# Convolution weights brought in unexpanded on 32 partitions and spread by ScalarE, in a group-norm and convolution kernel

## The chip, the cores and the metric

The kernel runs on one core of one Trainium2 chip. The metric is the device time of one execution in microseconds (us). The kernel before took 87.22 us, the median of three runs (86.58, 87.22 and 87.36). The profile shown below was taken from one more execution, which took 86.55 us; from its first to its last instruction it spans 84.8 us. TensorE, VectorE, ScalarE, GpSimd and SyncE are called PE, DVE, ACT, POOL and SP in the profile. A DMA is issued by an engine's queue (here SP's) and then moves data on the core's 16 DMA engines.

## The reference

The input `x` is 8 images of 32 channels and 128 x 128 pixels, float32. Each image is group-normalised (16 groups of two channels), convolved with a 3 x 3 weight of 32 x 32 channels, given a bias, and added to `x`. The convolution goes through a 256-point FFT, and its output window starts at offset 64:

```python
def _L0_conv_ref(x, weight, bias, stride, padding):
    # ... zero-pad x and weight to 256 x 256, multiply their FFTs, transform back to sp ...
    sh = (fft_H - out_h) // 2            # 64
    sw = (fft_W - out_w) // 2            # 64
    out = sp[:, :, sh:sh + out_h, sw:sw + out_w]
    return out + bias[None, :, None, None]

def _gn(v, G=16, eps=1e-5):              # mean and variance over two channels and all pixels
    # ...
    return ((g - m) / jnp.sqrt(s + eps)).reshape(v.shape)

x = x + _L0_conv_ref(_gn(x), L0_conv_weight, L0_conv_bias, 1, 1)
```

Output pixel (i, j) is therefore the full convolution at (i + 64, j + 64). It is different from the bias alone only for i and j up to 65, and it needs only the lower right corner of the image.

## The kernel before

The host splits every image by the parity of row and column: partition `q*32 + c`, with q = 2 x (row parity) + (column parity), holds channel c, as 64 x 64 values. So an image is a tile of 128 x 4096 floats, 2 MB. Eight such tiles stand in SBUF at once; every image has its own, is changed in place, and is stored from it. All loads and all stores are issued by SP, on one queue.

```python
    xts = [xpool.tile([P, H, W], F32, name=f"x{img}") for img in range(B)]
    wb_sb = cpool.tile([P, 4 * P + 1 + NSIGN], F32, name="wb_sb")   # 128 x 521 floats
    bias_sb = wb_sb[:, 4 * P : 4 * P + 1]
    signs = wb_sb[:, 4 * P + 1 :]
    for img in range(B):
        pieces = (4, 4) if img < 2 else (8,)       # images 0 and 1 in two halves
        # ...
            nc.sync.dma_start(xts[img][:, rows, :], x[img, :, rows, :])
        # ...
        if img == 0:
            nc.sync.dma_start(wb_sb, wb)
```

The 3 x 3 convolution of the parity-split image is four matmuls with 128 x 128 weight blocks, accumulated in PSUM, one for each pair (dr, dc) of shifts by 0 or 1. The blocks are built on the host: each tap of the 32 x 32 x 3 x 3 weight stands in several 32 x 32 squares of them, and the other squares are zero.

While data arrives, POOL makes a pattern and DVE makes from it the matrix `avg`, which averages over a group. PE runs matmuls into a spare bank before there is anything real to do (`keep_warm`). ACT loads its table with one early `Sqrt`. Then every image goes through these steps:

```python
    def take_stats(img, first, last):     # DVE, eight pieces of an image
        # ...
            nc.vector.bn_stats(stats[img][:, s, :], ...)

    def aggregate(img):                   # DVE, then two small ACT instructions
        nc.vector.bn_aggr(mv, stats[img].rearrange("p n s -> p (n s)"))
        nc.scalar.activation(terms[:, 0:NSIGN], signs, AF.Identity, scale=mv[:, 0:1])
        nc.scalar.activation(terms[:, NSIGN:], mv[:, 1:2], AF.Identity, bias=eps, scale=float(FFT * FFT))

    def group(img):                       # PE: averages over the group
        nc.tensor.matmul(ps_ms[img], avg, mvs[img], start=True, stop=True)

    def normalize(img):                   # small ACT and DVE steps, then g on ACT
        # ... square, var, std, rstd ...
            nc.scalar.activation(g[:, rows, :], xt[...], AF.Identity,
                                 bias=rstd[:, 1:2], scale=rstd[:, 0:1])

    def add_bias(img):                    # ACT: where the convolution is zero
        nc.scalar.activation(low, low, AF.Identity, bias=bias_sb)
        nc.scalar.activation(right, right, AF.Identity, bias=bias_sb)

    def multiply(img, n):                 # PE: four matmuls for a chunk of 11 rows
        # ...
            nc.tensor.matmul(ps[...], wb_sb[:, k * P : (k + 1) * P], g[...],
                             start=(k == 0), stop=(k == 3))

    def add(img, first, last):            # DVE: x + convolution + bias, in place
        nc.vector.scalar_tensor_tensor(..., scalar=bias_sb, ...)

    def store(img, first, last):
        nc.sync.dma_start(out[img, :, first:last, :], xts[img][:, first:last, :])

    keep_warm(0, 3)
    take_stats(0, 0, NSTAT)
    aggregate(0); group(0); keep_warm(0, 2); normalize(0); add_bias(0)
    take_stats(1, 0, NSTAT)
    for img in range(B):
        # ... multiply(img), aggregate/group/normalize/add_bias of img + 1,
        #     add and store of img - 1, statistics of img + 2 ...
    store(B - 1, N, H)
    add(B - 1, 0, 2)
    store(B - 1, 0, 2 * ROWS)
    add(B - 1, 2, NCHUNK)
    store(B - 1, 2 * ROWS, N)
```

The order of instructions on every engine is the order of the program. A DMA issue waits for the DMA eight issues earlier, whose completion counter it uses again.

Of the kernel before, what the change touches and what calls it, by code (L numbers as in the profile page):

```python
# [24 lines left out]
F32 = mybir.dt.float32  # L25
AF = mybir.ActivationFunctionType
ALU = mybir.AluOpType

P = 128
# [4 lines left out]
NSIGN = 8  # L34
# [3 lines left out]
def conv_preact_kernel(  # L38
# [6 lines left out]
    nc = tc.nc  # L45

    B, _, H, W = x.shape
    C = P // 4
    LO = (FFT - 2 * H) // 4 - 1
    N = H - LO  # L50
# [4 lines left out]
    cpool = ctx.enter_context(tc.tile_pool(name="const", bufs=1))  # L55
# [4 lines left out]


    xts = [xpool.tile([P, H, W], F32, name=f"x{img}") for img in range(B)]
    wb_sb = cpool.tile([P, 4 * P + 1 + NSIGN], F32, name="wb_sb")
    bias_sb = wb_sb[:, 4 * P : 4 * P + 1]
    signs = wb_sb[:, 4 * P + 1 :]
    for img in range(B):
        pieces = (4, 4) if img < 2 else (8,)
        first = 0
        for piece in pieces:
            rows = slice(first, first + piece * STATS)  # L70
            nc.sync.dma_start(xts[img][:, rows, :], x[img, :, rows, :])
            first += piece * STATS
        if img == 0:
            nc.sync.dma_start(wb_sb, wb)


    pair = cpool.tile([P, P // 2, 2], F32, name="pair")
# [6 lines left out]
        out=pair, in_=pair, pattern=[[2, P // 2], [0, 2]], base=1,  # L84
        channel_multiplier=-1, compare_op=ALU.is_ge, fill=0.0,
    )
    eps = cpool.tile([P, 1], F32, name="eps")
    nc.vector.memset(eps, EPS * FFT * FFT)
    pair2 = pair.rearrange("p a b -> p (a b)")
# [5 lines left out]

    warm = cpool.tile([P, 1], F32, name="warm")
    nc.scalar.activation(warm, eps, AF.Sqrt)  # L97

    gs = [cpool.tile([P, N, N], F32, name=f"g{k}") for k in range(2)]
    stats = [cpool.tile([P, NSTAT, 6], F32, name=f"stats{img}") for img in range(B)]  # L100
# [53 lines left out]
    def multiply(img, n):  # L154
        g = gs[img % 2]
        if n == 0:

            pss[img] = ps_conv.tile([P, NCHUNK, BANK], F32, tag="ps", name=f"ps{img}")
        ps = pss[img][:, n, 0 : ROWS * N].rearrange("p (r w) -> p r w", w=N)
        for k in range(4):  # L160
            dr, dc = k // 2, k % 2

            rows = min(ROWS, N - dr - n * ROWS)
            top = n * ROWS + dr
            nc.tensor.matmul(  # L165
                ps[:, 0:rows, 0 : N - dc], wb_sb[:, k * P : (k + 1) * P],
                g[:, top : top + rows, dc:N],
                start=(k == 0), stop=(k == 3),
            )
# [30 lines left out]
    for img in range(B):  # L200
        more = img + 1 < B
        multiply(img, 0)
        multiply(img, 1)
        if more:
            aggregate(img + 1)
        if img:
            add(img - 1, 0, NCHUNK)
            if img == 1:
                store(0, N, H)
                store(0, 0, N)  # L210
            else:
                store(img - 1, 0, H)
        if more:
            group(img + 1)
            normalize(img + 1)
            add_bias(img + 1)
        multiply(img, 2)
        if img + 2 < B:
            take_stats(img + 2, 0, NSTAT)
# [55 lines left out]
```

## Time and profile before

| What | Value |
|---|---|
| time, median of three | 87.22 us (86.58 to 87.36) |
| span of the profile | 84.8 us |
| PE busy | 66.1 us (78%), 218 instructions |
| DVE busy | 54.6 us (64%) |
| ACT busy | 48.5 us (57%), 82 instructions |
| POOL busy | 1.8 us (2%) |
| moved by DMA | 33.87 MB in 3172 packets, mean 399 GB/s |
| of it `wb_sb` | 260.5 KB, one DMA |

Shares of busy time are averages over the whole span. The profile also cuts the span into slices, and gives for each the busy share of every engine and of the DMA engines; it follows the chain of work that ended last back from the last instruction; and it lists how long each DMA took from its issue to its landing. A DMA's landing time holds its waiting in the queue too, behind what was issued earlier.

### The profile page before, as it was taken

How to read it: one execution, taken by the hardware profiler on the slowest of the kernel's cores; microseconds unless marked ns; L12 is line 12 of the kernel's file. 1: busy time of each engine (PE TensorE's matmuls, PEld its weight loads, DVE VectorE, ACT ScalarE, POOL GpSimd, SP SyncE). 2: the span in 40 equal slices, each digit the busy share in tenths (PEclk: the TensorE clock that was granted, in tenths of full speed). 3: DMA queues.
4: the chain of work that ended last, by engine and by line, in shares of the span. 5: the costliest groups of instructions: out<-in, count | busy, mean ns of one | idle time of the engine just before them, and what ended most of it. 6: DMA issues, size and time to landing. Idle time of an engine off the chain costs nothing.

```text
span 84.8 us, 732 instructions
## 1 busy us (share of the span) xinstructions
PE 66.1 (78%) x218; PEld 40.1 (47%) x218; DVE 54.6 (64%) x103; ACT 48.5 (57%) x82; POOL 1.8 (2%) x7
## 2 busy tenths in 40 slices
PE   0009968999999999999999999999999999500000
PEld 0014323666666666666666676666666666100000
DVE  0319938973998899699799969969992600420000
ACT  6000037984994897599489769948967980000000
POOL 6200000000000000000000000000000000000000
PEclk9999999999999999999999999999999999985555
DMA  2899999999999999999999999999999999999970
GB/s 39 294 425 413 435 429 471 417 448 409 448 394 456 409 433 421 440 409 433 317 404 426 472 417 448 409 456 402 456 409 448 417 448 417 433 417 402 414 318 17
DMA packets 3172, 33.87 MB, mean 399 GB/s; under 512 B 352, under 2 KB 352, under 8 KB 992
## 3 DMA queue, kind: packets, MB, share of 16 engines
q1 hardware_dynamic: 3168, 33.82, 95.1%
q8 instruction: 2, 0.03, 0.1%
q14 instruction: 2, 0.02, 0.0%
HBM read 17.04 MB, written 16.78 MB: 399 GB/s over the span
## 4 chain that ended last, share of the span: by engine, by line
PE 70%; DVE 8%; DMA 6%; ACT 2%; DVEq 1%; issue 0%
PE ps L165 68%; DMA x<-x_dram 6%; DVE stats L105 6%; PE ps_m L124 1%; DVE x L174 1%; ACT g L141 1%; DVEq L270 1%; DVE mv L113 0%; ACT std L136 0%; ACT terms L115 0%; ACT square L132 0%; ACT rstd L139 0%; ACT terms L116 0%; DVE rstd L138 0%; DVE var L133 0%
## 5 line engine op out<-in xcount | busy, mean ns | idle before, releaser
L165 PE MATMUL ps<-g,wb_sb 128*128 128x363 f32 (+1 forms) x192 | 58.7, 462 | 0.3 <-ACT g L141 0.3
L165 PEld LDWEIGHTS ps<-g,wb_sb 128*128 128x128 f32 x192 | 35.3, 189 | 20.5 <-ACT g L141 2.7
L105 DVE BATCH_NORM_STATS2 stats<-x 128x6 f32<-128x512 f32 x64 | 38.7, 677 | 2.7 <-DMA x<-x_dram 2.6
L150 ACT ACTIVATE x<-x,wb_sb 128x1984 f32<-128x1984 f32 x8 | 15.6, 1949 | 0.3
L174 DVE SCALAR_TENSOR_TENSOR x<-ps,wb_sb,x 128x1089 f32<-128x1089 f32 (+2 forms) x9 | 10.5, 1180 | 7.2 <-PE ps L165 7.2
L141 ACT ACTIVATE g<-x,rstd 128x396 f32<-128x396 f32 (+1 forms) x16 | 12.7, 838 | 0.3
L190 PE MATMUL ps_w<-x,avg 128*128 128x512 f32 x10 | 7.1, 864 | 6.2 <-DMA x<-x_dram 6.2
L152 ACT ACTIVATE x<-x,wb_sb 128x1023 f32<-128x1023 f32 x8 | 9.1, 1132 | 0.0
L115 ACT ACTIVATE terms<-wb_sb,mv 128x8 f32<-128x8 f32 x8 | 2.4, 301 | 10.9 <-DVE mv L113 10.9
L190 PEld LDWEIGHTS ps_w<-x,avg 128*128 128x128 f32 x10 | 2.5, 273 | 8.7 <-issue 8.7
L124 PEld LDWEIGHTS ps_m<-terms,avg 128*128 128x128 f32 x16 | 3.0, 190 | 3.4 <-ACT terms L116 1.9
L132 ACT ACTIVATE square<-ps_m 128x7 f32<-128x7 f32 x8 | 1.4, 177 | 5.2 <-PE ps_m L124 5.2
L133 DVE COPY var<-ps_m 128x1 f32<-128x1 f32 x8 | 1.3, 158 | 4.6 <-ACT square L132 4.6
L136 ACT ACTIVATE std<-var 128x1 f32<-128x1 f32 x8 | 2.4, 295 | 1.8 <-DVE var L133 1.8
L138 DVE RECIPROCAL rstd<-std 128x1 f32<-128x1 f32 x8 | 1.3, 164 | 2.9 <-ACT std L136 2.9
L113 DVE BATCH_NORM_AGGREGATE mv<-stats 128x2 f32<-128x48 f32 x8 | 3.0, 372 | 0.3
L139 ACT ACTIVATE rstd<-ps_m,rstd 128x1 f32<-128x1 f32 x8 | 2.1, 261 | 1.8 <-DVE rstd L138 1.8
L124 PE MATMUL ps_m<-terms,avg 128*128 128x9 f32 x16 | 2.4, 222 | 0.7 <-ACT terms L116 0.7
L116 ACT ACTIVATE terms<-mv,eps 128x1 f32<-128x1 f32 x8 | 2.2, 279 | 0.0
L97 ACT ACT_TABLE_LOAD x1 | 1.3, 1283 | 0.8 <-PEq L263 0.8
L132 ACT ACTIVATION_READ_ACCUMULATOR square<-ps_m 128x1 f32 x8 | 1.6, 194 | 0.0
L91 DVE TENSOR_TENSOR avg<-pair 128x64 f32<-128x64 f32 x1 | 0.2, 226 | 1.7 <-POOL pair L83 1.7
(11 smaller groups left out, 2.8 us busy)
## 6 DMA issues: line engine op xcount, KB each, us to landing
x<-x_dram SPq DMA_DIRECT2D x6, 2048.0 KB, 26.1
out_dram<-x SPq DMA_DIRECT2D x6, 2048.0 KB, 13.7
x<-x_dram SPq DMA_DIRECT2D x4, 1024.0 KB, 8.4
out_dram<-x SPq DMA_DIRECT2D x2, 992.0 KB, 21.2
out_dram<-x SPq DMA_DIRECT2D x1, 1056.0 KB, 22.4
out_dram<-x SPq DMA_DIRECT2D x1, 704.0 KB, 8.7
out_dram<-x SPq DMA_DIRECT2D x1, 352.0 KB, 9.1
wb_sb<-wb_dram SPq DMA_DIRECT2D x1, 260.5 KB, 7.5
```

The lines of the kernel that those rows point to most:

```text
L105: nc.vector.bn_stats(stats[img][:, s, :], xts[img][:, STATS * s : STATS * (s + 1), :].rearrange("p h w -> p (h w)"),)
L113: nc.vector.bn_aggr(mv, stats[img].rearrange("p n s -> p (n s)"))
L115: nc.scalar.activation(terms[:, 0:NSIGN], signs, AF.Identity, scale=mv[:, 0:1])
L124: nc.tensor.matmul(ps_ms[img], avg, mvs[img], start=True, stop=True)
L132: nc.scalar.activation(square, contrasts, AF.Square, accum_out=var[:, 0:1])
L136: nc.scalar.activation(std, var[:, 0:1], AF.Sqrt, bias=var[:, 1:2])
L141: nc.scalar.activation(g[:, rows, :], xt[:, LO + rows.start : LO + rows.stop, LO:W], AF.Identity, bias=rstd[:, 1:2], scale=rstd[:, 0:1],)
L150: nc.scalar.activation(low, low, AF.Identity, bias=bias_sb)
L152: nc.scalar.activation(right, right, AF.Identity, bias=bias_sb)
L165: nc.tensor.matmul(ps[:, 0:rows, 0 : N - dc], wb_sb[:, k * P : (k + 1) * P], g[:, top : top + rows, dc:N], start=(k == 0), stop=(k == 3),)
L174: nc.vector.scalar_tensor_tensor(part.rearrange("p (n r) w -> p n r w", r=ROWS), in0=pss[img][:, first:last, 0 : ROWS * N].rearrange("p n ...
L190: nc.tensor.matmul(ps_w, avg, piece, start=True, stop=True)
```

## The change

The weights, the biases and the sign patterns are no longer laid out on the host for 128 partitions. The host sends the weight as it is, input channel first (32 x 288 floats), and beside it for each of the four quarters of the partitions its column of biases and its eight columns of signs (32 x 36 floats): 32 rows of 324 floats, 41 KB in place of 260.5 KB. This is loaded once, on partitions 0 to 31, between the two halves of image 0 (before: after both). On the chip POOL fills a tile `w_sb` of 128 x 512 floats with zero. Then 20 ACT instructions, five for each quarter, copy the bias and sign columns and the taps to the quarter's partitions and to their places in the four blocks. They stand in ACT's order after the early `Sqrt` and ahead of image 0's first real step. The matmuls then read `w_sb`, and the bias and the signs come from the small tile `bs_sb`. The change is for moving fewer bytes.

```diff
-    wb_sb = cpool.tile([P, 4 * P + 1 + NSIGN], F32, name="wb_sb")
-    bias_sb = wb_sb[:, 4 * P : 4 * P + 1]
-    signs = wb_sb[:, 4 * P + 1 :]
+    wb_sb = cpool.tile([C, 9 * C + 4 * (1 + NSIGN)], F32, name="wb_sb")
     ...
             nc.sync.dma_start(xts[img][:, rows, :], x[img, :, rows, :])
+            if img == 0 and first == 0:
+                nc.sync.dma_start(wb_sb, wb)
             first += piece * STATS
-        if img == 0:
-            nc.sync.dma_start(wb_sb, wb)
     ...
+    w_sb = cpool.tile([P, 4 * P], F32, name="w_sb")
+    nc.gpsimd.memset(w_sb, 0.0)
     ...
+    bs_sb = cpool.tile([P, 1 + NSIGN], F32, name="bs_sb")
+    bias_sb, signs = bs_sb[:, 0:1], bs_sb[:, 1:]
+    taps = wb_sb[:, 0 : 9 * C].rearrange("p (a b o) -> p a b o", a=3, b=3)
+    w6 = w_sb.rearrange("p (dr dc r q o) -> p dr dc r q o", dr=2, dc=2, r=2, q=2)
+    places = {
+        0: ((0, slice(0, 1), slice(2, 3)), (1, slice(0, 2), slice(0, 2))),
+        1: ((0, slice(0, 2), slice(1, 3)), (1, slice(1, 2), slice(0, 1))),
+    }
+    for rin in range(2):
+        for cin in range(2):
+            q = 2 * rin + cin
+            to = slice(q * C, (q + 1) * C)
+            of = 9 * C + q * (1 + NSIGN)
+            nc.scalar.activation(bs_sb[to, :], wb_sb[:, of : of + 1 + NSIGN], AF.Identity)
+            for dr, r, a in places[rin]:
+                for dc, c, b in places[cin]:
+                    nc.scalar.activation(w6[to, dr, dc, r, c, :], taps[:, a, b, :], AF.Identity)
     ...
-                ps[:, 0:rows, 0 : N - dc], wb_sb[:, k * P : (k + 1) * P],
+                ps[:, 0:rows, 0 : N - dc], w_sb[:, k * P : (k + 1) * P],
     ...
-    blocks = np.zeros((2, 2, C, 2, 2, 2, 2, C), weight.dtype)
     ... the host's loops that filled the blocks ...
-                blocks.reshape(4 * C, 16 * C),
-                np.tile(np.asarray(L0_conv_bias).reshape(C, 1), (4, 1)),
-                signs,
+                weight.transpose(1, 2, 3, 0).reshape(C, 9 * C),
+                np.concatenate(
+                    [np.broadcast_to(np.asarray(L0_conv_bias).reshape(C, 1), (4, C, 1)),
+                     signs.reshape(4, C, NSIGN)],
+                    axis=2,
+                ).transpose(1, 0, 2).reshape(C, 4 * (1 + NSIGN)),
```

More of the change, by code (lines that the diff above doesn't have):

```diff
@@ L234 @@
     weight = np.asarray(L0_conv_weight)
-    blocks = np.zeros((2, 2, C, 2, 2, 2, 2, C), weight.dtype)
-    for dr, rin, rout in np.ndindex(2, 2, 2):
-        a = rout + 2 - 2 * dr - rin
-        for dc, cin, cout in np.ndindex(2, 2, 2):
-            b = cout + 2 - 2 * dc - cin
-            if 0 <= a <= 2 and 0 <= b <= 2:
-                blocks[rin, cin, :, dr, dc, rout, cout, :] = weight[:, :, a, b].T
     bits = [(-1.0) ** (np.arange(4 * C) // k % 2) for k in (2 * C, C, 1)]
```

## The prediction

> **What bounds the kernel now.** I read the chain of work that ended last first, because it names a bound, and then looked for what it leaves out.
>
> ```profile
> PE 70%; DVE 8%; DMA 6%; ACT 2%; DVEq 1%; issue 0%
> ...
> 63.71 9.53 PE ps L165 x32
> 73.24 0.02 issue
> 73.26 0.97 DVE x L174
> 74.24 0.50 DVEq L270
> ```
>
> The reader is to see that the shares add up to only 87%, and that the chain stops at 74.74 us in a span of 84.8. The last 10 us have no compute instruction in them: they are the last stores. So the next views are the slices and the busy time by stage (columns: stretch and its length; PE, PEld, DVE, ACT and POOL busy; the granted clock; the share of the DMA engines; GB/s).
>
> ```profile
> DMA  2899999999999999999999999999999999999970
> ...
> 4.00:42.00 38.00, 34.83 (x110) 20.44 (x111) 30.66 (x56) 24.25 (x44) 0.00 (x0) 1.00 1.01 425
> 44.00:82.00 38.00, 29.22 (x103) 18.40 (x102) 21.48 (x37) 21.28 (x33) 0.00 (x0) 0.92 1.01 428
> ...
> 78.00:80.00 2.00, 0.00 (x0) 0.00 (x0) 0.00 (x0) 0.00 (x0) 0.00 (x0) 0.50 0.99 418
> 80.00:82.00 2.00, 0.00 (x0) 0.00 (x0) 0.00 (x0) 0.00 (x0) 0.00 (x0) 0.50 1.00 411
> 82.00:84.00 2.00, 0.00 (x0) 0.00 (x0) 0.00 (x0) 0.00 (x0) 0.00 (x0) 0.50 0.18 69
> ```
>
> The DMA engines are full from about 4 us until 82 us, at 425 to 428 GB/s, in the half with the loads as in the half with the stores. PE is nearly as full from 14.5 to 73.2 us, but PE is not what the end waits for. The test is how long each late store stays in the queue:
>
> ```profile
> 63.81 0.33 SPq L182 DMA_DIRECT2D out_dram<-x  x1
> out_dram<-x SPq DMA_DIRECT2D x1, 2048.0 KB, 10.4
> ...
> out_dram<-x SPq DMA_DIRECT2D x1, 704.0 KB, 8.7
> ```
>
> The very first load, with an empty queue before it, took 5.2 us for 1024 KB, of which about 2.45 us is moving at 428 GB/s; some 2.8 us is the way there and back. A 2048 KB store alone would then take 4.9 + 2.8 = 7.7 us, and 704 KB 1.7 + 2.8 = 4.5 us. The real ones took 10.4 and 8.7 us, so they waited 2.7 and 4.2 us behind others. The other whole-image stores took 11.4 us and more. So computing could be up to about 2.7 us later everywhere, and the DMA engines would still never run dry. **The bound is the stream of bytes, 33.87 MB, on the DMA engines**; everything else fits inside it.
>
> **What the Trainium skill says.** Four places bear on this. "DMA: Bandwidth & Descriptors", "Where 436 GB/s comes from", puts the ceiling of the 16 engines at 435 GB/s; the trace's 425 and 428 GB/s are 98% of that, so nothing but fewer bytes shortens the stream. The same page, "Why a DMA increments its semaphore by 16 and not by 1", says that a DMA is divided over the largest number of engines, up to 16, that divides its slowest dimension: 128 rows are then 8 per engine, and 32 rows are 2 per engine. No view here shows the division. Its section "Queues, rings and completion order" says that each engine takes its queue's descriptors in order, so a load put earlier delays all behind it by its own length; the landings of the trace are in the order of issue. "ScalarE: Activation LUTs", "What ACT_TABLE_LOAD costs", gives an activation of N elements per partition as 186 ns + 0.833 ns x N when scale and bias are immediate, 93 ns more for each operand that is a pointer, and 93 ns of overlap back to back. The trace agrees:
>
> ```profile
> L150 ACT ACTIVATE x<-x,wb_sb 128x1984 f32<-128x1984 f32 x8 | 15.6, 1949 | 0.3
> ...
> L132 ACT ACTIVATE square<-ps_m 128x7 f32<-128x7 f32 x8 | 1.4, 177 | 5.2 <-PE ps_m L124 5.2
> ```
>
> The rule gives 279 + 1653 = 1932 ns for the first, with one pointer (measured 1949), and 192 ns for the second, with none (177). In the timeline the two instructions that make `terms` start at 11.47 and 11.68 us while the first is 0.30 us long: they overlap by 0.09 us.
>
> **The change, part by part.**
>
> *Fewer bytes.* The old load is 128 x 521 x 4 = 266,752 bytes, the new one 32 x 324 x 4 = 41,472. What the old one cost the stream is read from SP's issues, because the last three loads wait for the landing of the DMA eight issues earlier:
>
> ```profile
> 6.06 0.33 SPq L71 DMA_DIRECT2D x<-x_dram  x1
> 8.55 0.33 SPq L71 DMA_DIRECT2D x<-x_dram  x1
> 9.20 0.33 SPq L71 DMA_DIRECT2D x<-x_dram  x1
> ```
>
> They were released by the first half of image 0, its second half, and `wb_sb`. The second half took 2.49 us, `wb_sb` 0.65 us. The new load has a quarter of the rows per engine, each 1296/2084 = 0.62 as long: 0.65 x 0.25 x 0.62 = 0.10 us; rows of 1296 bytes are a little dearer per byte, so I take 0.12 us. **Saved on the stream: 0.65 - 0.12 = 0.53 us.** By bytes alone it is 0.225 MB / 428 GB/s = 0.53 us too. This lies on the path that sets the end, and comes back in full.
>
> *The load's new place.* It now goes ahead of image 0's second half, which lands about 0.12 us later, at 8.67 in place of 8.55 us. DVE finishes the first half's statistics at 8.54 us (6.07 + 2.47 in the chain), so all of the front of the computation may start 0.12 us later. The slack of 2.7 us takes that: cost at the end 0.
>
> *The zero fill on POOL.* A fill of 128 x 128 took 0.205 us; four times that is at most 0.8 us, from 2.6 to 3.4 us. ACT needs it only when the weights land. Cost 0.
>
> *Twenty copies on ACT.* A quarter has one copy of 9 elements and four of 32, 64, 64 and 128: 297 elements, 1188 in all. By the rule above a copy takes 93 ns + 0.833 ns x N in a row: 20 x 0.093 + 1188 x 0.000833 = 1.86 + 0.99 = 2.85 us. They begin when the small load lands, at about 6.06 + 0.12 = 6.2 us, and end at 9.1 us. ACT is idle there: its `terms` instruction waits until DVE's aggregate ends at 11.45 us (its longest idle stretch is 9.2 us). **All 2.85 us lie in that gap, with 2.4 us to spare. Cost 0.**
>
> *Sum.* -0.53 us, everything else beside it. 87.22 - 0.53 = 86.69; I say **86.7 us**, 0.6% less.
>
> **The rivals.**
>
> First, *ACT comes too late*. With no overlap and with pointer operands, a copy is 279 ns + 0.833 ns x N: 5.58 + 0.99 = 6.57 us, ending at 12.8 us, 1.3 us after the aggregate. The first matmul would start 1.3 us later, and so would everything on PE. The overlap in the trace speaks against it. Even so the slack is 2.7 us before and about 2.2 us after (the stream being 0.5 us shorter), so the time would still be near 86.7 us. Only if the copies took over 7.4 us would the end move; at 10 us in all, about 89 us.
>
> Second, *PE is the real bound*, as the chain's 70% suggests. Then fewer bytes bring nothing, the front is 0.1 us later, and the time is 87.3 us. Against it stand the 10 us of stores after PE's end, and the 10.4 us that a store waits.
>
> Third, *the saved bytes are filled elsewhere*: there is a dip to about 300 GB/s at 41 to 43 us, where the stream turns from loads to stores, and the DMA engines do not all end together (69 GB/s from 82 to 84 us). If the small load is put on fewer engines, say four rows on each of eight, those eight save 0.65 - 0.24 = 0.41 us only. That makes 86.8 us.
>
> **Range and chances.** The effect is 0.4 to 0.65 us by the steps above. The three runs before differ by 0.78 us among themselves, which is more than the effect, and a median of three can be off by half of that. So 86.1 to 87.3 us should hold it eight times in ten. Faster by 2% would need 1.74 us, three times what the load's whole removal could give: 0.02. Slower by 2% needs the first rival at its worst: 0.03. Within 2%: 0.95.
>
> **What would show each step right or wrong.** In the profile after: 96 packets fewer (3172 to about 3076) and 33.64 MB; SP's load that waits for `wb_sb` issued at about 6.2 us and the one that waits for image 0's second half at 8.67 us; the third landing thus 0.5 us sooner than before; 20 copies on ACT of mean 0.24 us that end by 9.1 us; an idle ACT until DVE's aggregate; PE's first convolution at 14.5 to 14.7 us and its last end at 73.2 to 73.5 us; the late stores' landing times 0.5 to 0.7 us shorter than 8.7 and 10.4; the span at 84.3 us. I am wrong if PE's end moves by over 2 us, if the copies are longer than 0.35 us each, or if the stream's dip at the turn from loads to stores becomes longer.

## The result, and the profile after

The changed kernel takes **85.91 us**, the median of six runs (85.57 to 86.13), against 87.20 us before (86.58 to 87.36). The ratio is 0.9865, with a 95% interval of 0.9824 to 0.9906: 1.3 us less, where 0.53 us was predicted. All ratios below leave out executions over 1.5% above their kernel's fastest; as the kernel before spreads by more than that, its ratios are nearer to 1 than those of the medians, and I give both.

The page of the changed kernel shows the smaller load as expected, and DMA engines that are as full as before:

```profile
span 83.9 us, 752 instructions
...
DMA  2899999999999999999999999999999999999990
...
DMA packets 3075, 33.63 MB, mean 401 GB/s; under 512 B 352, under 2 KB 384, under 8 KB 896
```

The 20 copies, in the groups by form (number, then busy us, mean ns of one, idle before and its releaser):

```profile
L118 ACT ACTIVATE w_sb<-wb_sb 32x64 f32<-32x64 f32 x8 | 1.7, 238 | 0.0
L118 ACT ACTIVATE w_sb<-wb_sb 32x128 f32<-32x128 f32 x4 | 1.2, 292 | 0.0
L118 ACT ACTIVATE w_sb<-wb_sb 32x32 f32<-32x32 f32 x4 | 0.8, 211 | 0.0
L115 ACT ACTIVATE bs_sb<-wb_sb 32x9 f32<-32x9 f32 x4 | 0.8, 210 | 4.2 <-DMA wb_sb<-wb_dram 4.2
```

The last of them and what follows, in ScalarE's timeline:

```profile
9.07 0.70 ACT L118 ACTIVATE w_sb<-wb_sb 32x128 f32<-32x128 f32 x4
11.75 0.30 ACT L136 ACTIVATE terms<-bs_sb,mv 128x8 f32<-128x8 f32 x1 [1.98 <-DVE mv L134]
```

They run from 6.46 to 9.77 us and ScalarE then sits idle for 1.98 us: hidden. The late stores, shown for before at 10.4 and 8.7 us, are the surprise. Their issue in the timeline, and their landing in the table of DMAs:

```profile
64.15 0.33 SPq L203 DMA_DIRECT2D out_dram<-x  x1
```

```profile
out_dram<-x SPq DMA_DIRECT2D x1, 2048.0 KB, 9.0
...
out_dram<-x SPq DMA_DIRECT2D x1, 704.0 KB, 7.4
```

Both are issued 0.34 us later than before (64.15 and 74.64 us) and land 1.1 and 1.0 us earlier. That is more than the stream was shortened by. The end of the span, by stage (the last two numbers are the share of the DMA engines and GB/s; one engine of 16 is 0.06), first before:

```profile
82.00:83.00 1.00, 0.00 (x0) 0.00 (x0) 0.00 (x0) 0.00 (x0) 0.00 (x0) 0.50 0.31 124
83.00:84.00 1.00, 0.00 (x0) 0.00 (x0) 0.00 (x0) 0.00 (x0) 0.00 (x0) 0.50 0.04 14
```

and after:

```profile
81.00:82.00 1.00, 0.00 (x0) 0.00 (x0) 0.00 (x0) 0.00 (x0) 0.00 (x0) 0.50 0.72 287
82.00:83.00 1.00, 0.00 (x0) 0.00 (x0) 0.00 (x0) 0.00 (x0) 0.00 (x0) 0.50 0.07 28
```

The last stretch shown holds about one engine's work after (0.07) and less before (0.04): the end is set by the **last** of 16 engines, not by the stream as a whole. The trace marks the completion of each DMA on each engine, 16 marks a DMA. Below, the mean mark is the mean over the 16 marks of the last store, and the lag is how far the last of them comes after it. The marks of the last store have a mean of 82.75 us before and 82.18 after (0.57 less, the forecast's 0.53), and the last of them comes 1.13 us after that mean before, and 0.72 after. So there are two gains: the bytes, and an end with less lag. The second one is what the experiments are about.

### The profile page after: what moved, and what is told of

The parts are those of the page before. It is cut to its first block, busy times and chain, and to the rows that moved or that the text cites. A ratio compares the mean times of both kernels' runs of the same rounds, so it can differ in the third digit from the quotient of the medians.

```text
span 83.9 us, 752 instructions
## 1 busy us (share of the span) xinstructions
PE 66.3 (79%) x218; PEld 40.1 (48%) x218; DVE 54.5 (65%) x103; ACT 51.8 (62%) x102; POOL 2.3 (3%) x8
## 2 busy tenths in 40 slices
DMA packets 3075, 33.63 MB, mean 401 GB/s; under 512 B 352, under 2 KB 384, under 8 KB 896
## 4 chain that ended last, share of the span: by engine, by line
PE 70%; DVE 8%; DMA 7%; ACT 2%; issue 1%; DVEq 1%; ACTq 0%
PE ps L186 69%; DMA x<-x_dram 7%; DVE stats L126 6%; PE ps_m L145 2%; DVE x L195 1%; ACT g L162 1%; DVEq L287 1%; DVE mv L134 0%; ACT std L157 0%; ACT terms L136 0%; ACT square L153 0%; ACT rstd L160 0%; ACT terms L137 0%; DVE rstd L159 0%; DVE var L154 0%
## 5 line engine op out<-in xcount | busy, mean ns | idle before, releaser
L186 PE MATMUL ps<-g,w_sb 128*128 128x363 f32 (+1 forms) x192 | 58.7, 462 | 0.4 <-ACT g L162 0.4
L186 PEld LDWEIGHTS ps<-g,w_sb 128*128 128x128 f32 x192 | 35.3, 189 | 20.6 <-ACT g L162 1.6
L171 ACT ACTIVATE x<-x,bs_sb 128x1984 f32<-128x1984 f32 x8 | 15.6, 1950 | 0.3
L195 DVE SCALAR_TENSOR_TENSOR x<-ps,bs_sb,x 128x1089 f32<-128x1089 f32 (+2 forms) x9 | 10.5, 1179 | 7.2 <-PE ps L186 7.2
L173 ACT ACTIVATE x<-x,bs_sb 128x1023 f32<-128x1023 f32 x8 | 9.1, 1132 | 0.0
L136 ACT ACTIVATE terms<-bs_sb,mv 128x8 f32<-128x8 f32 x8 | 2.4, 301 | 3.7 <-DVE mv L134 3.7
L115 ACT ACTIVATE bs_sb<-wb_sb 32x9 f32<-32x9 f32 x4 | 0.8, 210 | 4.2 <-DMA wb_sb<-wb_dram 4.2
L118 ACT ACTIVATE w_sb<-wb_sb 32x64 f32<-32x64 f32 (+2 forms) x16 | 2.8, 244 | 0.0
```

Source lines behind the costliest of these rows:

```text
L118: nc.scalar.activation(w6[to, dr, dc, r, c, :], taps[:, a, b, :], AF.Identity)
L186: nc.tensor.matmul(ps[:, 0:rows, 0 : N - dc], w_sb[:, k * P : (k + 1) * P], g[:, top : top + rows, dc:N], start=(k == 0), stop=(k == 3),)
L195: nc.vector.scalar_tensor_tensor(part.rearrange("p (n r) w -> p n r w", r=ROWS), in0=pss[img][:, first:last, 0 : ROWS * N].rearrange("p n ...
```

## The experiments

Bytes, place of the load and ScalarE's longer program change together in this diff. The theories: all of the gain is **bytes**; the rest comes from the load's **place**; the rest comes from the **program**, whose instructions are fetched through the same DMA engines. Medians of the kernel before were 87.03, 87.20, 86.96 and 87.02 us in the four sets of runs.

**Repeats.** Both kernels once more, unchanged.

> The kernel before, run once more as it is, for a second trace of it. Every theory: ratio 1.00, 87.2 us. If the last DMA engine's lag is an accident of one execution, its second trace ends its stores at another time than 83.9 us; if it belongs to the program, the instruction fetch at about 71 us and the end near 83.9 us come again.

> The changed kernel once more as it is. All theories: near 85.9 us, if the first measurement was typical. Its trace shows whether the mean of the 16 engines' last completions (82.18 us in the first trace, 82.75 before) and the lag of the last engine behind that mean (0.72 us, against 1.14 before) come again: the mean should, to 0.1 us; by the theory that the lag is an accident of each execution, the lag should lie elsewhere between 0.7 and 1.7 us.

Before: 87.09 us, ratio 0.9998 (0.9967 to 1.003). Its one trace, of an execution of 87.38 us, has the last mark at 84.50 us and no instruction fetch near 71 us, so neither came again; nothing below is built on so long an execution. After: 85.88 us, ratio 0.9888 (0.9829 to 0.9947). Its mean mark is 82.17 us and its lag 0.78 us. The mean came again to 0.01 us and the lag to 0.06, so in the changed kernel neither is an accident of one execution.

**Old size at the new place, with the copies.**

```diff
-    wb_sb = cpool.tile([C, 9 * C + 4 * (1 + NSIGN)], F32, name="wb_sb")
+    wb_sb = cpool.tile([P, 521], F32, name="wb_sb")     # rows and columns beyond 32 x 324 are unused
     ... the copies read wb_sb[0:C, ...]; the host pads the array with zeros ...
```

> The changed kernel, but its one load has the old size again, 128 rows of 521 floats (only 32 x 324 of them are used), at the new place. Bytes alone (all of the 1.3 us come from the bytes): 87.2 us, the gain is gone. Bytes and program (0.53 us from bytes, the rest from another instruction stream and the lag of the last DMA engine): 86.4 to 86.5 us. Place (the rest comes from the load's new place): 86.4 us too; the run with the load moved alone tells these two apart.

86.49 us, ratio 0.9985 (0.996 to 1.001); mean mark 82.66, lag 0.98 us. Against the changed kernel's 85.9 us the bytes are worth 0.6 us, and by the medians something else is worth the other 0.5. By the ratio alone the bytes would carry all but 0.15%. The mean mark is on the side of before.

**No copies, small load.** All matmuls run, on zero weights; bias and signs are ones.

```diff
-    for rin in range(2): ...          # the 20 copies
+    nc.gpsimd.memset(bs_sb, 1.0)
```

> The changed kernel without the 20 copies: the small load stays, the weights stay zero and the bias and sign columns are filled with one by POOL, so the convolution is left out in value but every matmul runs. ScalarE's program has its old length. Bytes alone or place: 85.9 us as the changed kernel, since the copies are hidden. Bytes and program: 86.6 us, with an instruction fetch late in the trace as in the kernel before.

86.19 us, ratio 0.9922 (0.9888 to 0.9957), mean mark 82.24, lag 1.01 us: between the two expectations. Leaving the copies out gains nothing, as it should if they are hidden, and the mean follows the bytes.

**Program alone.**

```diff
     nc.scalar.activation(warm, eps, AF.Sqrt)
+    spare = cpool.tile([P, C], F32, name="spare")
+    for _ in range(20):
+        nc.scalar.activation(spare, avg[:, 0:C], AF.Identity)
```

> The kernel before with 20 extra ScalarE instructions (128 x 32, into a tile nobody reads) after the early Sqrt, done before image 0's statistics end. Bytes and place are those of before. Bytes alone or place: 87.2 us. Bytes and program: 86.4 to 86.5 us, with no instruction fetch near 71 us and a last DMA engine that lags less (1.2 us in place of 1.65 us from first to last engine).

87.02 us, ratio 1.0013 (0.998 to 1.0046): the length of ScalarE's program by itself does nothing to the time. That theory, in this form, fell.

**Place alone, and size alone.**

```diff
+            if img == 0 and first == 0:
+                nc.sync.dma_start(wb_sb, wb)
             first += piece * STATS
-        if img == 0:
-            nc.sync.dma_start(wb_sb, wb)
```

> The kernel before with its 260.5 KB load issued between the two halves of image 0, nothing else changed. Place theory (the load's place takes some 0.5 us off the last engine's lag, whatever its bytes): 86.5 us, as the changed kernel with the big load had. Program theory (the longer ScalarE program does it, together with the place or by how instruction fetches fall): 87.0 us as before. The mean of the last completions stays at 82.7 us by both.

The same edit the other way round, in the changed kernel:

> The changed kernel with its small load issued after both halves of image 0, where the old load stood. Bytes theory: mean of the last completions 82.2 us as with the small load elsewhere. Place theory: the gain of the bytes alone remains, 87.0 - 0.55 = 86.5 us. Program theory: 85.9 us, as the changed kernel. The copies start at about 8.8 us and end at 12.1 us, which makes the first matmul 0.4 us later; by the slack of the stores that costs nothing.

The large load moved: 86.47 us, ratio 0.996 (0.993 to 0.999), mean mark 82.76 as with any large load. So the place seems to give 0.6 us by the medians and 0.35 by the ratio. It is also the time of the old size at the new place (86.49 us), so the copies and ScalarE's longer program add nothing to it; the two ratios differ with the runs of the kernel before that they divide by. The small load at the old place: 86.06 us, ratio 0.9915 (0.9882 to 0.9949). The place is worth little there. This one shows a new thing: its copies start at 8.82 us and end at 12.14, behind the aggregate, the first convolution comes at 16.69 us (14.89 in the changed kernel) with a granted clock of half speed in between, and PE ends at 76.55 us, 3 us late. By stage:

```profile
64.00:66.00 2.00, 2.00 (x8) 1.29 (x7) 1.97 (x5) 1.75 (x3) 0.00 (x0) 1.00 0.98 418
66.00:68.00 2.00, 2.00 (x10) 1.33 (x9) 1.34 (x3) 0.94 (x5) 0.00 (x0) 1.00 0.52 221
68.00:70.00 2.00, 2.00 (x9) 1.25 (x8) 0.58 (x2) 1.85 (x4) 0.00 (x0) 1.00 1.09 459
```

The DMA engines wait there for a store that isn't computed yet, and all start level again: the lag at the end is 0.08 us, the mean mark 83.29. Three microseconds of PE cost 0.15 us, because the wait was paid by engines that had time.

**How much slack there is.**

```diff
+    spare = cpool.tile([P, P], F32, name="spare")
+    for _ in range(30):
+        nc.scalar.activation(spare, avg, AF.Identity)    # between the copies and image 0's terms
```

> The changed kernel with 30 more ScalarE instructions (128 x 128 into a tile nobody reads) after the 20 copies, about 6 us, so that image 0's first real step and all of PE's work come some 4 us later. It asks how much slack there really is. Stream bound with the slack of the prediction (2.7 us before, 1.3 us left in the changed kernel by the 9.0 us of its shortest store against 7.7 us): about 4 - 1.3 = 2.7 us longer, 88.6 us. Stream bound with the slack counted for the last engine (its data queue ends 3.7 us after that store's issue, of which 1 us is the way to the first byte): 4 - 2.75 = 1.25 us longer, 87.2 us, with all 16 engines ending closely together, as all wait for the same store. PE bound: 4 us longer, 89.9 us.

92.92 us, ratio 1.0683 (1.0604 to 1.0762). The instructions took longer than I had reckoned, 10.2 us in all, or 0.34 us each in a row. They all write one tile; that each waits for the one before it is argued, not shown. The end of the chain, and two stages:

```profile
73.07 9.53 PE ps L190 x32
82.62 0.97 DVE x L199
```

```profile
62.00:64.00 2.00, 2.00 (x9) 1.22 (x8) 2.00 (x4) 2.00 (x2) 0.00 (x0) 1.00 0.92 393
64.00:66.00 2.00, 2.00 (x10) 1.34 (x9) 1.74 (x3) 1.07 (x5) 0.00 (x0) 1.00 0.00 0
```

From 64 to 66 us no byte moves: here PE is the bound. PE ends at 82.60 us, 9.02 later than in the changed kernel (73.58), and the span is 6.5 us longer, 90.4 against 83.9. The slack is the difference, 2.5 us. The prediction had 2.2.

**What a later front does.** Moving the large load ahead of image 0's second half also makes that half land later, at 9.07 in place of 8.55 us, and the convolutions start at 15.04 in place of 14.52. Perhaps that, not the place, was the gain. What meets the stream at a time set by PE is PE's instruction fetch. The queues marked `instruction` move three blocks in mid-kernel: two of 8 KB, when DVE and ACT have run some 47 and 52 instructions, and one of 16 KB at PE's 95th to 100th matmul record, at 38 to 40 us. Some kernels have a second one of 16 KB at about 70 us: it stands in the trace of the kernel before, at 71.16 us, and in neither of the changed kernel's. Before and after, from the two pages (packets, MB, share of 16 engines):

```profile
q8 instruction: 2, 0.03, 0.1%
```

```profile
q8 instruction: 1, 0.02, 0.1%
```

The first block comes just ahead of the turn from loads to stores, which ends at about 43 us. The Trainium skill's page "Runtime: NRT & Kernel Launch", section "Instruction fetch mechanics", says that an engine's instructions come in 16 KiB blocks by a DMA queue of its own, and that the cost is mostly hidden. The trace agrees for PE (16,384 bytes); the two smaller blocks are 8,192 bytes each and share one queue. Whether the cost is hidden here is the question. I held the loads as they were and shifted only the front, later in the kernel before, and sooner in both:

```diff
+        if img == 0:
+            for k in range(1):                    # range(2) in the second
+                spare = cpool.tile([P, 512], F32, name=f"spare{k}")
+                nc.scalar.activation(spare, wb_sb[:, 0:512], AF.Identity, scale=mv[:, 0:1])
         terms = spool.tile([P, NSIGN + 1], F32, tag="terms", name=f"terms{img}")
```

> The kernel before with one extra ScalarE instruction of 512 elements between image 0's aggregate and its terms, so that all of PE's convolutions start about 0.6 us later (15.0 us in place of 14.4 to 14.5); loads, bytes and places as before. Timing theory (what the moved load changed is when PE's 16 KB instruction fetch, 23.5 us after its first convolution, meets the turn of the DMA stream from loads to stores): 86.5 us, as with the load moved. Place theory (the order of the loads itself): 87.1 us, as before. Both: mean of the 16 engines' last completions 82.7 us.

> The same with two such instructions, so about 1.2 us later. Timing theory: 86.5 us again, or less. Place theory: 87.1 us. The slack measured so far (PE's end 3.0 us later cost 0.15 us, 9.0 us later cost 7.0 us) covers 1.2 us.

```diff
-    take_stats(0, 0, NSTAT)
+    take_stats(0, 0, 6)              # and bn_aggr of image 0 over six pieces
```

> The changed kernel, but image 0's statistics are taken from six of its eight pieces, so that everything after starts 1.2 us sooner (PE's first convolution at 13.6 us). The last 16 of the image's 64 rows are left out of its mean and variance. Timing theory: the instruction fetch comes at about 37 us, as far ahead of the turn as in the kernel before, and part of the gain is lost: 86.2 to 86.6 us, with the last engine 1.2 us or more behind the mean. Place theory: 85.9 us, the last engine 0.7 to 0.8 us behind the mean, as in the two traces of the changed kernel.

> The kernel before with image 0's statistics from six of eight pieces, so everything after starts 1.2 us sooner (PE's first convolution at 13.3 us). Timing theory: no better than before, 87.1 us or above, the last engine 1.4 us or more behind the mean. Place theory: 87.1 us. It tells whether the loss of the kernel before lies at one meeting of fetch and turn, or at all early ones.

Later is faster and sooner is slower. In the kernel before: one instruction more, 86.44 us (ratio 0.9956, 0.9931 to 0.998); two, 86.65 (0.9971, 0.9945 to 0.9996); 1.2 us sooner, 87.61 (1.0079, 1.0049 to 1.0109). In the changed kernel 1.2 us sooner, 86.32 us (0.9919, 0.9884 to 0.9955) against 85.88. The two added instructions shifted the convolutions by more than meant, to 16.10 us, which the theory allows. **The load's place is not needed: the same 0.6 us come from a front that starts later.** The ends of the kernel before with the front sooner, by stage:

```profile
82.00:83.00 1.00, 0.00 (x0) 0.00 (x0) 0.00 (x0) 0.00 (x0) 0.00 (x0) 0.50 0.33 130
83.00:84.00 1.00, 0.00 (x0) 0.00 (x0) 0.00 (x0) 0.00 (x0) 0.00 (x0) 0.50 0.08 34
84.00:85.00 1.00, 0.00 (x0) 0.00 (x0) 0.00 (x0) 0.00 (x0) 0.00 (x0) 0.50 0.03 11
```

and with it later:

```profile
82.00:83.00 1.00, 0.00 (x0) 0.00 (x0) 0.00 (x0) 0.00 (x0) 0.00 (x0) 0.50 0.29 113
83.00:84.00 1.00, 0.00 (x0) 0.00 (x0) 0.00 (x0) 0.00 (x0) 0.00 (x0) 0.50 0.01 3
```

Until 83 us they are alike; in the first, one engine still has work beyond 84 us, and in the second nearly none is left after 83.

**Is it the fetch?** A front that moves takes the fetch along, but also PE, DVE and the stores. So I tried to move the fetch alone, by the number of instructions that PE runs ahead of the convolutions.

```diff
-    keep_warm(0, 3)
+    keep_warm(0, 1)                  # fetch later: four records fewer
```

```diff
-    keep_warm(0, 3)
+    keep_warm(0, 2)                  # fetch sooner: six records more
+    for _ in range(4):
+        nc.tensor.matmul(ps_w[:, 0:1], avg, xts[0][:, 0, 0:1], start=True, stop=True)
```

> The kernel before with two of the three first warming matmuls left out, so PE's program is shorter by four records ahead of the convolutions and its 16 KB instruction fetch, taken at about the 96th record, comes some 1.2 us later (39.2 us or more), while the convolutions start when they did (14.4 us, if the clock stays up). Fetch theory: 86.5 us, the last engine 0.9 to 1.1 us behind the mean. Timing of PE or of the stores, without the fetch: 87.1 us as before.

> The kernel before with one of the three first warming matmuls left out and four one-column ones added, six records more, so the fetch comes some 1.8 us sooner (about 36.2 us) with the convolutions at their time. Fetch theory: 87.1 to 87.6 us, the last engine 1.4 to 2 us behind the mean. Timing of PE or of the stores: 87.1 us.

> The changed kernel with two of the first warming matmuls left out: fetch at about 40 us, convolutions at 14.8 us. Fetch theory: 85.9 us or a little less, the last engine 0.7 us behind the mean. Timing of PE or of the stores: 85.9 us.

> The changed kernel with six records more ahead of the convolutions: fetch at about 37.1 us, convolutions at 14.8 us. Fetch theory: 86.3 us as when everything ran 1.2 us sooner, the last engine 1.2 to 1.5 us behind the mean. Timing of PE or of the stores: 85.9 us, 0.75 us behind the mean. This run tells the two apart most sharply.

Before: fetch later 86.48 us (ratio 0.9934, 0.991 to 0.9958), fetch sooner 87.56 us (1.009, 1.0063 to 1.0117). Changed kernel: later 85.69 us (0.988, 0.9837 to 0.9924), sooner 86.69 us (0.9979, 0.995 to 1.0008). Changing the warming matmuls also slowed PE at the start, so that in the chain of work the convolutions began 0.9 to 1.8 us later than planned; this took the same direction in all four. So "fetch later" by itself is one more later front: its fetch comes 24.1 us after the first convolution in both kernels, against 25.1 (before) and 24.0 us (changed) without the edit. The edit to fetch sooner does separate the two, with 19.6 and 20.6 us. In the changed kernel the convolutions of the two runs begin at 16.65 and 16.52 us, the fetches at 40.72 and 37.16 us, and the times are 1.0 us apart. In the kernel before, fetch sooner begins the convolutions at 15.38 us, later than the moved load did (15.04), and yet is 1.1 us slower than it. The front does not explain that; the fetch, or what else the changed warming matmuls do, must. The fetch is found in the queue view of a short stretch, here 34.9 to 36 us of the kernel before with the fetch sooner (packets, MB, share of 16 engines):

```profile
q8 instruction: 1, 0.02, 6.2%
```

6.2% is one engine of 16, for the whole stretch of 1.1 us. With the front later the same block is found from 39.9 us on. All kernels whose stores never waited for PE, in the order of that time:

| Kernel | load, KB | 16 KB fetch begins, us | mean of the last marks, us | last engine behind it, us | median, us |
|---|---|---|---|---|---|
| before, fetch sooner | 260 | 35.00 | 82.70 | 1.61 | 87.56 |
| before, front sooner | 260 | 37.60 | 82.84 | 1.95 | 87.61 |
| before, 20 idle instructions | 260 | 38.02 | 82.66 | 1.44 | 87.02 |
| changed, old size | 260 | 38.79 | 82.66 | 0.98 | 86.49 |
| before, load moved | 260 | 39.53 | 82.76 | 1.02 | 86.47 |
| before | 260 | 39.58 | 82.75 | 1.13 | 87.0 to 87.2 |
| before, front later | 260 | 39.93 | 82.66 | 0.89 | 86.44 |
| before, fetch later | 260 | 40.26 | 82.67 | 0.97 | 86.48 |
| before, front later still | 260 | 40.51 | 82.56 | 0.96 | 86.65 |
| changed, front sooner | 41 | 37.31 | 82.04 | 1.53 | 86.32 |
| changed | 41 | 38.85 | 82.18 | 0.72 | 85.9 |
| changed, no copies | 41 | 39.09 | 82.24 | 1.01 | 86.19 |

Two readings. The mean is 82.56 to 82.84 us with the large load and 82.04 to 82.24 with the small one, whatever else is done. The lag is 1.4 us and more where the fetch begins by 38.02 us, and 0.7 to 1.1 where it begins from 38.79 us on. Each row is one traced execution; that of the kernel before was one of 86.55 us, faster than its median. The changed kernel with the fetch moved is not in the table, because its stores waited for PE (mean marks 82.55 and 82.76 us). Its two traced executions, 86.16 and 86.26 us, are also hardly apart, and their lags are 0.94 us with the fetch later and 0.73 with it sooner, where the fetch theory expected 0.7 and 1.2 to 1.5; only the medians and ratios speak for it.

The packets show more. Over 99% of them outside the turn begin 3 or 4 ns before another one ends, and every engine moves the same sizes in the same order, so they can be joined into 16 chains, one for each engine. **In all twelve traces of the table the engine that served PE's 16 KB block at 35 to 41 us ends last or next to last.** It ends 1.65 to 2.26 us behind the middle of the 16 in the four traces with a fetch by 38.02 us, where it is always the last, and 0.72 to 1.12 us behind it in the eight others. In the trace of the kernel before, the last engine (its data ends at 83.51 us) served the second block, at 71.16 us, and the next (83.22 us) the first one. In that of the changed kernel, the last (82.58 us) served an 8 KB block and the next (82.49 us) PE's.

## Why the prediction was wrong

- **Bytes: right.** Predicted 0.53 us off the stream; the mean of the last marks fell by 0.57. Packets and megabytes came as said but for one packet (3075 and 33.63, said 3076 and 33.64), and image 0's second half landed at 8.76 us (said: 8.67).
- **The copies: right in kind.** 3.31 us in place of 2.85, ending at 9.77 in place of 9.1 us: 166 ns for each in a row, where the rule that the prediction takes from the Trainium skill's page "ScalarE: Activation LUTs", section "What ACT_TABLE_LOAD costs", gave 143; the measurement decides. They lie in ScalarE's gap. Rival one did not happen in the changed kernel; with the load at its old place it did, at little cost.
- **Slack: right.** 2.5 us measured, 2.2 said. Rival two, PE as the bound, begins beyond that, and only there.
- **The step that failed** is "everything else beside it" in the sum, and in it "all of the front of the computation may start 0.12 us later ... cost at the end 0". The front started 0.37 us later (14.89 against 14.52 us). I asked only whether a later PE could hurt the stores, and not what else moves on the DMA engines that are the bound. Instruction blocks do, and the engine that serves PE's ends last or next to last. I had seen that the engines do not end together and took their lag as fixed: the third rival names it and gives it no term. The lag fell from 1.13 to 0.72 us in the traced executions, 0.4 us on top of the bytes; by the medians 0.5 to 0.7 us came off beyond them.
- **What shortened the lag is shown in part.** In the traced executions PE's first fetch did not come later in the changed kernel: it began at 38.85 and 38.89 us, against 39.58 before. What differs there is the second block, which the changed kernel's traces do not have; in the kernel before its engine ended last, 0.29 us behind the next. The second block is not all of it: with 20 idle instructions it does not come near 71 us either, the first comes at 38.02 us, and the lag is 1.44 us. The trace of the kernel before is of an execution of 86.55 us; what makes its typical execution, of 87.1 us, longer stays open. Moving its front or its fetch gave medians from 86.44 to 87.61 us.
- **Not told apart:** why a fetch by 38 us costs its engine more than one from 38.8 us on. The block itself takes 1.0 to 1.1 us, which is about what the later ones cost. At the turn, from 40 to 43 us, 18 of the kernel before's 61 packets of 16 KB take over 0.8 us, up to twice their usual 0.61 us; that an engine held up ahead of the turn loses one such packet more is argued, not shown. No run did without the fetch.

## What to carry to other kernels

Where the DMA engines are full from end to end, a saved byte is worth its share of the stream at once, and compute instructions put in a gap are free up to a slack that can be read from how long the late stores wait in the queue. But the end is the last engine's, so look at how unevenly the engines end, and at what else runs on them: here the engine that had also moved PE's instructions was always last or next to last. Shifts of the front or the fetch moved the time by 1.1 us, twice what the bytes gave, so test a small change against the same kernel with its front shifted before the whole gain is put down to it.

## What the runs showed that I had not expected

- A 16 KB fetch of PE's instructions occupied one DMA engine for 1.0 to 1.1 us, against 0.61 us for a data packet of the same size, and the engine that served it ended last or next to last in all twelve traces of the table. Shifting it by changing PE's warming matmuls moved the medians by 1.0 to 1.1 us.
- With two warming matmuls fewer at 6 us, the next ones took 0.94 us each in place of 0.49 and the first convolution came 1.7 us later (16.18 against 14.52 us), though the granted clock in that stretch reads 1.00.
- ScalarE instructions that all write one tile took 0.34 us each in a row (30 of 128 elements in 10.2 us); copies to different places took 0.17 us.
